# A last expert stage whose stored sums, bias, norms and buffers are arranged anew

## The chip, the cores and the metric

The program runs on one core of a Trainium2 chip. The core has TensorE (PE, matrix products into PSUM), VectorE (DVE), ScalarE (ACT), GpSimd (POOL) and SyncE (SP), each with an instruction queue of its own that it works through in order; they meet at semaphores, and data come and go by DMA, which here SP and POOL issue. The metric is the time of one execution on the device in microseconds (us), as the median of several runs. Before the change it is 5069.14 us, the median of 3 runs from 5067.45 to 5076.32.

## The reference

The input x is (2, 256, 64, 64), in two layers: a state-space scan block over 4096 tokens; then a forward and a backward scan block on normalised tokens, and a mixture of eight experts with a router. Only the end of it is touched:

```python
t = t + ffn(layer_norm(t))            # t: (2 batches, 4096 tokens, 256 channels)
# ffn(x):
feat = mean(x, axis=0)                # over the two batches
w = softmax(feat @ Wr + br)           # (tokens, 8), shared by the batches
h = relu(bn1(x @ W1[e] + b1[e]))      # for each of the 8 experts e
h = relu(bn2(h @ W2[e] + b2[e]))
y = h @ Wo[e] + bo[e]
ffn = sum over e of w[:, e] * y[e]
```

## The kernel before

**Tiling.** Tokens go in 8 chunks of T = 512 for each of 2 batches; channels lie in KC = 2 halves of 128 partitions. One [128, 2, 512] float32 tile (512 KB) is a chunk of one batch. A *pair* is (batch b, chunk i, expert e): three layers, each of 4 products of a 128x128 weight with 512 columns (8 matmul instructions in the profile).

**The scans (up to L1137).** A slot plan, written out by hand in `Slots`, gives every piece of work a slot and a queue; `in_order` ties each engine to the traced order. In the slots where PE and ACT have room, `experts` and `emit_experts` compute pairs ahead of time: the three layers of L989, evictions by ACT at L1000 and, for the last layer, the copy of L998 into a tile `eu`, which SP or, at the end, POOL stores to DRAM as `u` (L1019). `features` stores the normalised chunk as `nf_dram` (L891). Of the 128 pairs 86 are stored this way: all of batch 0, and in batch 1 chunks 7 and 6 whole and experts 0 to 5 of chunk 5 (`first[b, i]` is the number of stored experts). Only (batch 1, chunk 0) has no stored norm. The tiles of this work have the tags `ew0` to `ew2` (weights), `en`, `eh1`, `eh2` and `eu` in the pool `wk` of the scans.

**The last stage (from L1140)** opens new pools when those of the scans are closed: `mw` for the weights of all experts, `mk` for the rest, `ps_o` for the sums in PSUM, and four PSUM banks (`psm`) for all other products. It computes the 42 pairs that are left:

- `rest` lists the chunks that have pairs left, in order 4, 3, 2, 1, 0, 5 (8 pairs each, 2 in chunk 5); `whole` is 7, 6.
- The main loop (L1347) does a pair's first two layers (`layer`, L1283, evicted by ACT at L1287), multiplies the hidden tile of the pair before by the router's weights (`weigh`, DVE, L1294), and adds the last layer of the pair three before into PSUM (`last_layer`, L1302). After a chunk's last pair DVE adds PSUM to x (L1307) and SP stores it (L1257).
- `routes(i)` is the router of a chunk: `load_n` (POOL's DMA, L1168), `layer_norm` where no norm is stored, `both` (POOL adds the norms of both batches, L1190), `logits` (PE, L1197, then a softmax on DVE and ACT), `spread` (PE transposes, ACT copies, POOL stores the weights and loads them back over all partitions as `wb`, L1226 and L1228).
- `sums(i)`: load x (L1238); `bias`, a product of the router's weights with `bo` (L1245), copied by ACT (L1246) and added to x of both batches by POOL (L1248); then for each stored result a load (L1252), a product with `wb` (L1253) and an add to x (L1254), both on DVE.
- `side[i]` holds a chunk's stored sums and the routers of the chunks to come, dealt out evenly over that chunk's own pairs:

```python
upto = -(-len(work) // (count[i] - done[i] + 1))
for fn in work[:upto]:
    fn()
```

So chunk 5's 14 stored sums come with its two pairs, at the very end.

Of the kernel before, what the change touches and what calls it, by code (L numbers as in the profile page):

```python
# [134 lines left out]
def hybrid_kernel(ctx: ExitStack, tc: tile.TileContext, a: dict, out: bass.AP):  # L135
# [41 lines left out]
    wr = const.tile([P, KC, E], F32, name="wr")  # L177
    br = const.tile([P, E], F32, name="br")
# [10 lines left out]

    with ExitStack() as st:  # L190
# [7 lines left out]
        psp = st.enter_context(tc.tile_pool(name="psp", bufs=3, space=PSUM))  # L198
# [16 lines left out]
        def load_weights(job, tag, s0):  # L215
# [4 lines left out]
            def weight(key, home, shape, name):  # L220
# [4 lines left out]
                elif key == "x":  # L225
                    w["x_dt"] = wk.tile([P, KC * C], F32, tag="ew2", name=f"{name}_{tag}")
                    w[key] = w["x_dt"][:, : nj * XC].rearrange("p (j n) -> p j n", j=nj)
                else:
                    w[key] = wk.tile(shape, F32, tag=NARROW_W[home], name=f"{name}_{tag}")
# [226 lines left out]
        def prepare(i):  # L456
# [8 lines left out]
            def of_chunk(key, j, bufs, home):  # L465
                if not ahead:
                    ck[key, j] = wk.tile([P, T], F32, tag=key, name=f"{key}_{tag}_{j}", bufs=bufs)
                else:
                    if j == 0:
                        ck[key] = wk.tile([P, KC, T], F32, tag=home, name=f"{key}_{tag}")  # L470
# [11 lines left out]
            def scaled():  # L482
                ck["nx"] = wk.tile([P, KC, T], F32, tag="en", name=f"nx_{tag}")
# [6 lines left out]
            def load_x():  # L490
                ck["x"] = wk.tile([P, KC, T], F32, tag="eh1", name=f"x_{tag}")
# [407 lines left out]
        def scales():  # L899
# [3 lines left out]
            def load():  # L903
# [5 lines left out]
                nc.sync.dma_start(wr, a["Wr"].rearrange("(k p) e -> p k e", p=P))  # L909
                nc.sync.dma_start(br, a["br"].to_broadcast([P, E]))  # L910

            def shift():
# [5 lines left out]
                nc.vector.tensor_scalar(wr, wr, 1.0 / NB, None, ALU.mult)  # L918
# [63 lines left out]
        def emit_experts(put):  # L982
            ew, before = {}, {}

            def layer(x, dst, l, m, e, key):
# [8 lines left out]
                def act():  # L994
                    if dst not in key:
                        key[dst] = wk.tile([P, KC, T], F32, tag=f"e{dst}", name=f"e{dst}_{key['tag']}")
                    if l == 2:
                        nc.scalar.copy(key[dst][:, m, :], key["ps", l, m])  # L998
# [8 lines left out]
            def load_w(l, e, tag):  # L1007
                ew[l] = wk.tile([P, KC, C], F32, tag=f"ew{l}", name=f"ew{l}_{tag}")
# [4 lines left out]
            def load_n(b, c):  # L1013
                n[b, c] = wk.tile([P, KC, T], F32, tag="en", name=f"en_{b}{c}")
# [49 lines left out]
        def chunk_stats(n, s0):  # L1064
            v = {}

            def load():
                v["x"] = wk.tile([P, KC, T], F32, tag="eu", name=f"xst_{n}")
# [71 lines left out]
    with ExitStack() as st:  # L1140
# [3 lines left out]
        psp = st.enter_context(tc.tile_pool(name="psm", bufs=4, space=PSUM))  # L1144
# [11 lines left out]
        rest.sort(key=lambda i: sum(first[b, i] for b in range(NB)))  # L1156

        def load_n(i):

            if (0, i) in n:  # L1160
                return
            for b in range(NB):
                n[b, i] = mk.tile([P, KC, T], F32, tag="n", name=f"n_{i}{b}", bufs=6)
# [5 lines left out]

        def layer_norm(i):  # L1170
# [305 lines left out]
```

## Time and profile before

One execution was profiled. It lasted 5072.22 us, of which the span of the instructions is 5070.5 us.

| | us |
|---|---|
| median of the runs | 5069.14 |
| profiled execution / its span | 5072.22 / 5070.5 |
| busy in the span: PE, DVE, ACT, POOL | 4247.6, 4581.4, 3609.1, 4409.8 |
| last matmul of the scans' experts ends | 4504.4 |
| first matmul of the last stage | 4517.58 |
| busy 4518 to 4985 (467 us): PE, DVE, ACT, POOL | 442.84, 241.86, 138.72, 69.31 |
| busy 4985 to 5071 (86 us): PE, DVE, ACT, POOL | 54.75, 44.79, 12.12, 5.75 |
| stored sums, DVE: 86 products, 86 adds | 1.22 each, median |
| hidden tile times weights, DVE: 42 | 1.22 each, median |

The profile names an instruction by its line in the kernel, the engine, what it writes and reads (`out<-in`), and gives the idle time of its engine before it and who ended that. The page cuts the span into 40 slices of 127 us; each digit is the busy share of a slice in tenths. The last stage is the last four and a half of them.

### The profile page before, as it was taken

To read this page: it belongs to the slowest core of one execution; us is meant where nothing else is said; L and a number is where in the kernel's file an instruction comes from. 1 tells how busy PE (TensorE), PEld (TensorE's weight loads), DVE (VectorE), ACT (ScalarE), POOL (GpSimd) and SP (SyncE) were. 2 spreads that over 40 slices of the span, in tenths; PEclk is the share of its full clock that TensorE was granted. 3 is DMA by queue.
4 is the path that set the end of the run, shared out by engine and by line. 5 is a ranking of instruction groups with operands and counts; after the bars stand their busy time and mean duration, and the time that the engine had idled before them with its cause. 6 is when DMAs were issued, how large, how long until landed. Compare 5 with 4: busy or idle time off the path is not lost. (4 is left out here: it accounts for less than half of the span.)

```text
span 5070.5 us, 47370 instructions
## 1 busy us (share of the span) xinstructions
PE 4247.6 (84%) x14920; PEld 1478.8 (29%) x14920; DVE 4581.4 (90%) x3096; ACT 3609.1 (71%) x7319; POOL 4409.8 (87%) x1442
## 2 busy tenths in 40 slices
PE   5667787787777899989999888898868999888997
PEld 1222222222222333333333333333222333334443
DVE  6998999999999999999999999999999999946635
ACT  5677777777776877877787888878777788742231
POOL 5998999999999999999999999999999999931110
PEclk8788889899888999999999999999889999999998
DMA  5455444444444444457675555544444554544533
GB/s 189 155 172 180 160 159 160 146 155 155 170 167 155 162 171 165 160 198 246 233 243 185 175 184 178 188 161 172 140 160 167 175 177 158 175 168 175 199 112 137
DMA packets 333947, 873.15 MB, mean 172 GB/s; under 512 B 36408, under 2 KB 111936, under 8 KB 291712
## 3 DMA queue, kind: packets, MB, share of 16 engines
q1 hardware_dynamic: 329408, 842.73, 48.4%
q0 software_dynamic: 4288, 27.40, 1.4%
q8 instruction: 118, 1.93, 0.2%
q14 instruction: 133, 1.09, 0.1%
HBM read 671.17 MB, written 198.84 MB: 172 GB/s over the span
## 5 line engine op out<-in xcount | busy, mean ns | idle before, releaser
L737 POOL TENSOR_TENSOR bq<-rxdt,bc 128x2048 f32<-128x2048 f32 x640 | 2892.7, 4541 | 17.3 <-DMA rxdt<-xdtd 8.3
L747 ACT ACTIVATE da<-rdt,w_a 128x512 f32<-128x512 f32 x2560 | 1757.3, 686 | 110.3 <-DVE bq L773 63.9
L773 DVE TENSOR_TENSOR_SCAN da<-da,h_state,bq 128x1024 f32<-128x1024 f32 x664 | 1558.0, 2346 | 55.3 <-ACT da L747 44.7
L798 POOL TENSOR_TENSOR bq<-bq,bc 128x2048 f32<-128x2048 f32 (+1 forms) x280 | 1180.0, 4214 | 22.5
L773 DVE TENSOR_TENSOR_SCAN bq<-da,h_state,bq 128x1024 f32<-128x1024 f32 x456 | 1059.5, 2339 | 23.7 <-ACT da L747 23.7
L806 PE MATMUL y<-bq,stack 128*32 128x512 f32 x5120 | 741.9, 665 | 275.3 <-POOL bq L798 251.5
L782 DVE TENSOR_TENSOR bq<-da,bc 128x1024 f32<-128x1024 f32 x760 | 926.3, 1219 | 15.7
L989 PE MATMUL e<-eh,ew 128*128 128x512 f32 x1376 | 671.6, 622 | 63.9 <-DMA ew<-in_Wo 17.0
L792 ACT COPY h_state<-da 128x2 f32<-128x2 f32 x759 | 119.3, 157 | 634.1 <-DVE bq L782 632.3
L758 ACT ACTIVATE bq<-h_state,bq,a 128x1 f32<-128x1 f32 x1120 | 430.2, 384 | 2.7 <-POOL bq L737 2.0
L989 PEld LDWEIGHTS e<-eh,ew 128*128 128x128 f32 x1376 | 250.7, 194 | 475.9 <-issue 239.9
L806 PEld LDWEIGHTS y<-bq,stack 128*32 128x32 f32 x5120 | 140.1, 116 | 820.2 <-POOL bq L798 359.7
L450 PE MATMUL z<-nx,w_in 128*128 128x512 f32 x640 | 329.1, 643 | 58.1 <-DVE nx L414 21.2
L523 PE MATMUL conv<-xs,w_conv 64*64 64x512 f32 x2560 | 330.1, 602 | 23.5 <-ACT xs L507 21.3
L989 PE MATMUL e<-en,ew 128*128 128x512 f32 x688 | 323.8, 604 | 22.9 <-DVE fcen L886 15.8
L450 PE MATMUL xs<-nx,w_in 128*128 128x512 f32 x640 | 317.3, 625 | 21.1 <-DVE xc L536 7.9
L1287 ACT ACTIVATE h<-hp,of,sc 128x512 f32<-128x512 f32 x168 | 130.4, 777 | 252.2 <-PE hp L1283 235.6
L838 PE MATMUL o<-sz,w_out 128*128 128x512 f32 x640 | 298.3, 605 | 0.0
L1000 ACT ACTIVATE eh<-e,of,sc 128x512 f32<-128x512 f32 x344 | 259.3, 767 | 44.1 <-PE e L989 43.9
L590 POOL TENSOR_TENSOR xdt<-sp,xc 128x512 f32<-128x512 f32 x160 | 203.3, 1275 | 46.0 <-DVE sp L586 45.8
L773 DVE TENSOR_TENSOR_SCAN da<-da,bq 128x1024 f32<-128x1024 f32 x96 | 219.4, 2285 | 3.8 <-ACT da L747 2.2
L1248 POOL TENSOR_TENSOR x<-x,bi 128x1024 f32<-128x1024 f32 x16 | 37.2, 2338 | 188.8 <-DMA x<-t_dram 108.0
(141 smaller groups left out, 4924.1 us busy)
## 6 DMA issues: line engine op xcount, KB each, us to landing
rxdt<-xdtd SPq DMA_DIRECT2D x160, 1024.0 KB, 6.6
rdt<-dtd SPq DMA_DIRECT2D x160, 1024.0 KB, 6.5
bc<-bcd SPq DMA_DIRECT2D x384, 256.0 KB, 3.2
ew<-in_W SPq DMA_DIRECT2D x172, 256.0 KB, 5.0
u<-u SPq DMA_DIRECT2D x86, 512.0 KB, 4.3
u<-eu SPq DMA_DIRECT2D x82, 512.0 KB, 4.3
dtd<-sp SPq DMA_DIRECT2D x160, 256.0 KB, 3.5
xdtd<-xdt SPq DMA_DIRECT2D x160, 256.0 KB, 3.4
```

Source lines behind the costliest of these rows:

```text
L450: nc.tensor.matmul(ps, job.matrices["in", half][:, k, j * P : (j + 1) * P], rhs, start=(k == 0), stop=(k == KC - 1),)
L523: nc.tensor.matmul(v[r][64 * col : 64 * col + 64, :], job.matrices["conv"][rows, 2 * jp + j, k, :], ck["xs", jp][rows, j, k : k + T] if k ...
L737: nc.gpsimd.tensor_tensor(bq[g], ck["rxdt", j], over_groups(ck["bc", 0, sg]), ALU.mult)
L747: nc.scalar.activation(da[g, h][:, k, :], cks[i]["rdt", j][:, q, :], AF.Exp, scale=steps[i][0].w["a"][:, j, q * SG + sg : q * SG + sg + 1],)
L758: nc.scalar.activation(bq[g][:, q, 0:1], job.h[:, j, sg, q : q + 1], AF.Identity, scale=cks[i]["a0", j][:, h, sg : sg + 1], bias=bq[g][:, ...
L773: nc.vector.tensor_tensor_scan(b if on_pool(g, h) else d, d, b, job.h[:, j, sg, 2 * h : 2 * h + 1] if c else 0.0, ALU.mult, ALU.add,)
L782: nc.vector.tensor_tensor(bq[g][:, two, :], d, cks[i]["bc", 1, sg].rearrange("p (o t) -> p o t", o=1).to_broadcast([P, 2, T]), ALU.mult,)
L798: nc.gpsimd.tensor_tensor(b, b, cks[i]["bc", 1, sg].rearrange("p (o t) -> p o t", o=1).to_broadcast([P, groups, T]), ALU.mult,)
L806: nc.tensor.matmul(y[i, j][q * CG : (q + 1) * CG, :], stack, bq[g][:, q, :], start=False, stop=(sg == SG - 1),)
L838: nc.tensor.matmul(v[m], job.w["out"][:, j, m * P : (m + 1) * P], ck["sz", j], start=False, stop=(j == job.nj - 1),)
L989: nc.tensor.matmul(ps, ew[l][:, k, m * P : (m + 1) * P], key[x][:, k, :], start=(k == 0), stop=(k == KC - 1),)
L1000: nc.scalar.activation(key[dst][:, m, :], key["ps", l, m], AF.Relu, bias=of[:, l, e, m : m + 1], scale=sc[:, l, e, m : m + 1],)
```

## The change

Buffers: a pool `ep` and the PSUM pool `psp` (3 banks) are opened outside the scans and serve both parts. The tiles with the tags `ew*`, `en`, `eh*` and `eu` move into `ep` everywhere (one such line is shown). The last stage takes its stored results (`summand`), the sum of norms (tag `en`) and the last expert's weights (tags `ew*`) from these tiles; `layer` takes its three banks from `psp`, and the router's products share one bank (`psm`).

Output bias: at the eviction of a stored result, `bo` is added by ACT (`bo_col`). For pairs of the last stage, a product of the router's weights with `bo`, zero where an expert is stored, opens the sum in PSUM (`late_bias`). The step `bias` goes.

Sum of norms: except for the first chunk, it is loaded by POOL's DMA from `nf_dram` of one batch, and the other batch's is added by an accumulating DMA. Batch 0's norms are no longer loaded by themselves. `wr` and `br` are loaded in the last stage, on POOL's queue, not in the scans.

Order: `rest` becomes 4, 3, 2, 1, 5, 0. All stored sums stand in one list with costs (2.5 for a sum, 0.3 for a load of x) that is dealt out over all 42 pairs; routers stand in a second list, a step or two to a pair. x is loaded for one batch at a time, at its first sum, or before the add of PSUM. A chunk is stored once its last part is added. Weights are loaded three tiles to a pair, not six. `wb` has three buffers, not two.

```diff
+
+    ep = ctx.enter_context(tc.tile_pool(name="ep", bufs=1))
+    psp = ctx.enter_context(tc.tile_pool(name="psp", bufs=3, space=PSUM))
+    bo_col = const.tile([P, E, KC], F32, name="bo_col")
...
-                    w["x_dt"] = wk.tile([P, KC * C], F32, tag="ew2", name=f"{name}_{tag}")
+                    w["x_dt"] = ep.tile([P, KC * C], F32, tag="ew2", name=f"{name}_{tag}")
...
-                nc.sync.dma_start(wr, a["Wr"].rearrange("(k p) e -> p k e", p=P))
-                nc.sync.dma_start(br, a["br"].to_broadcast([P, E]))
+                nc.sync.dma_start(bo_col, a["bo_col"])
...
-                        key[dst] = wk.tile([P, KC, T], F32, tag=f"e{dst}", name=f"e{dst}_{key['tag']}")
+                        key[dst] = ep.tile([P, KC, T], F32, tag=f"e{dst}", name=f"e{dst}_{key['tag']}")
                     if l == 2:
-                        nc.scalar.copy(key[dst][:, m, :], key["ps", l, m])
+                        nc.scalar.activation(
+                            key[dst][:, m, :], key["ps", l, m], AF.Identity, bias=bo_col[:, e, m : m + 1]
+                        )
...
-        psp = st.enter_context(tc.tile_pool(name="psm", bufs=4, space=PSUM))
+        psm = st.enter_context(tc.tile_pool(name="psm", bufs=1, space=PSUM))
...
-        rest.sort(key=lambda i: sum(first[b, i] for b in range(NB)))
+        rest.sort(key=lambda i: (len([b for b in range(NB) if (b, i) not in featured]), sum(first[b, i] for b in range(NB))))
...
         def load_n(i):
 
-            if (0, i) in n:
-                return
             for b in range(NB):
-                n[b, i] = mk.tile([P, KC, T], F32, tag="n", name=f"n_{i}{b}", bufs=6)
+                if first[b, i] == E and i != rest[0]:
+                    continue
+                n[b, i] = mk.tile([P, KC, T], F32, tag="n", name=f"n_{i}{b}", bufs=4)
                 if (b, i) in featured:
                     src = nf_dram[b][:, i, :, :]
                 else:
                     src = t_dram[b][:, :, i * T : (i + 1) * T]
                 nc.gpsimd.dma_start(n[b, i], src)
 
+        def summand(name):
+            homes.append(homes.pop(0))
+            return ep.tile([P, KC, T], F32, tag=homes[-1], name=name)
+
+        homes = ["eh1", "eh2", "eu"]
...
             for b in range(NB):
-                if (b, i) in featured:
+                if (b, i) in featured or (b, i) not in n:
...
         def both(i):
-            n["sum", i] = mk.tile([P, KC, T], F32, tag="nm", name=f"nm_{i}", bufs=1)
-            nc.gpsimd.tensor_tensor(n["sum", i], n[0, i], n[1, i], ALU.add)
+            n["sum", i] = ep.tile([P, KC, T], F32, tag="en", name=f"nm_{i}")
+            if i == rest[0]:
+                nc.gpsimd.tensor_tensor(n["sum", i], n[0, i], n[1, i], ALU.add)
+                return
+            alone = [b for b in range(NB) if (b, i) in featured]
+            for b in alone:
+                nc.gpsimd.dma_start(
+                    n["sum", i], nf_dram[b][:, i, :, :],
+                    accum_op=ALU.bypass if b == alone[0] else ALU.add,
+                )
+            for b in range(NB):
+                if b not in alone:
+                    nc.gpsimd.tensor_tensor(n["sum", i], n["sum", i], n[b, i], ALU.add)
...
-            wb[i] = mk.tile([P, E, T], F32, tag="wb", name=f"wb_{i}")
+            wb[i] = mk.tile([P, E, T], F32, tag="wb", name=f"wb_{i}", bufs=3)
...
         def routes(i):
-            return [lambda: load_n(i), lambda: layer_norm(i), lambda: both(i), lambda: logits(i), lambda: spread(i)]
-
+        def load_x(b, i):
+            if (b, i) in x:
+                return
+            x[b, i] = mk.tile([P, KC, T], F32, tag="x", name=f"x_{i}{b}", bufs=6)
+            nc.sync.dma_start(x[b, i], t_dram[b][:, :, i * T : (i + 1) * T])
 
         def add_early(b, i, e):
-            u = mk.tile([P, KC, T], F32, tag="u", name=f"u_{b}{i}_{e}", bufs=3)
+            u = summand(f"u_{b}{i}_{e}")
...
+        left = {}
+
+        def added(b, i):
+            left[b, i] -= 1
+            if not left[b, i]:
+                store(b, i)
+
         def sums(i):
 
-            work = [lambda: load_x(i), lambda: bias(i)]
+            work = []
             for b in range(NB):
-                work += [lambda b=b, e=e: add_early(b, i, e) for e in range(first[b, i])]
-                if first[b, i] == E:
-                    work.append(lambda b=b: store(b, i))
+                left[b, i] = first[b, i] + (first[b, i] < E)
+                for e in range(first[b, i]):
+                    if not e:
+                        work.append((0.3, lambda b=b: load_x(b, i)))
+                    work.append((2.5, lambda b=b, e=e: (add_early(b, i, e), added(b, i))))
             return work
 
-        bo = mw.tile([E, C], F32, name="bo")
-        we = {}
-        order = sorted(range(E), key=lambda e: e < first[NB - 1, rest[0]])
+        def late_bias(k):
+            if k not in bo:
+                bo[k] = mw.tile([E, C], F32, name=f"bo_{k}")
+                if k:
+                    nc.vector.memset(bo[k], 0.0)
+                nc.sync.dma_start(bo[k][k:, :], a["bo"][k:, :])
+            return bo[k]
+
+        bo, we = {}, {}
+        order = list(range(E))
+        order = order[first[NB - 1, rest[0]] :] + order[: first[NB - 1, rest[0]]]
+        kept = [(name, e) for e in order[-1:] for name in ("W1", "W2", "Wo")]
...
@@ -1297,15 +1327,21 @@
             begins, ends = (e == [p[2] for p in pairs if p[:2] == (b, i)][k] for k in (0, -1))
             if begins:
                 y[b, i] = ps_o.tile([P, KC, T], F32, tag="y", name=f"y_{i}{b}")
+                for m in range(KC):
+                    nc.tensor.matmul(
+                        y[b, i][:, m, :], late_bias(first[b, i])[:, m * P : (m + 1) * P], wts[i],
+                        start=True, stop=False,
+                    )
             for m in range(KC):
                 for k in range(KC):
                     nc.tensor.matmul(
                         y[b, i][:, m, :], we["Wo", e][:, k, m * P : (m + 1) * P], h[:, k, :],
-                        start=(begins and k == 0), stop=(ends and k == KC - 1),
+                        start=False, stop=(ends and k == KC - 1),
                     )
             if ends:
+                load_x(b, i)
                 nc.vector.tensor_tensor(x[b, i], y[b, i], x[b, i], ALU.add)
-                store(b, i)
+                added(b, i)
...
+        chunks = rest[:1]
+        for k in range(max(len(rest), len(whole))):
+            chunks += rest[k + 1 : k + 2] + whole[k : k + 1]
+        starts_at = {i: min(k for k, p in enumerate(pairs) if p[1] == i) for i in rest}
+        ends_at = {i: max(k for k, p in enumerate(pairs) if p[1] == i) for i in rest}
+        ahead = [(cost, fn, i) for i in chunks for cost, fn in sums(i)]
+        total = sum(item[0] for item in ahead)
+        todo = [(i, fn) for i in chunks[1:] for fn in routes(i)]
+
+        load_n(chunks[0])
+        wr = mw.tile([P, KC, E], F32, name="wr")
+        br = mw.tile([P, E], F32, name="br")
+        nc.gpsimd.dma_start(wr, a["Wr"].rearrange("(k p) e -> p k e", p=P))
+        nc.gpsimd.dma_start(br, a["br"].to_broadcast([P, E]))
+        nc.vector.tensor_scalar(wr, wr, 1.0 / NB, None, ALU.mult)
...
-        nc.sync.dma_start(bo, a["bo"])
+        late_bias(first[NB - 1, rest[0]])
         layer_norm(rest[0])
         both(rest[0])
-        for i in whole[:1] + rest[1:2]:
+        for i in rest[1:2]:
...
+        weighed, loaded = -1, [2]
+
+        def free(i):
+
+            k = chunks.index(i) - 3
+            if k < 0:
+                return True
+            old = chunks[k]
+            return all(item[2] != old for item in ahead) and ends_at.get(old, -1) <= weighed
+
+        def load_ahead(at):
+            while loaded[0] < len(rest):
+                old = rest[loaded[0] - 2]
+                if ends_at[old] >= at or ("sum", old) not in n:
+                    break
+                load_n(rest[loaded[0]])
+                loaded[0] += 1
+
+        def route_on():
+            i, fn = todo[0]
+            if i in rest and not any((b, i) in n for b in range(NB)):
+                return False
+            if len(todo) > 1 and todo[1][0] == i or free(i):
+                fn()
+                todo.pop(0)
+                return True
+            return False
+
+        def finish_route(i):
+            while i not in wb:
+                if not route_on():
+                    if ahead[0][2] in wb:
+                        ahead.pop(0)[1]()
+                    else:
+                        weigh_next()
+
+        def weigh_next():
+            nonlocal weighed
+            weighed += 1
+            b, i, e = pairs[weighed]
+            finish_route(i)
+            weigh(b, i, e, hs[weighed])
+
+        hs, spent = {}, 0.0
         for at, (b, i, e) in enumerate(pairs):
-            for name, k in weights[: 6 if at else 4]:
+            for name, k in weights[: 3 if at else 4]:
                 load_w(name, k)
-            weights = weights[6 if at else 4 :]
+            weights = weights[3 if at else 4 :]
+            if at and i != rest[0]:
+                finish_route(i)
             h = layer(n[b, i], 0, e, f"{i}_{e}_{b}")
-            h = layer(h, 1, e, f"{i}_{e}_{b}")
+            hs[at] = layer(h, 1, e, f"{i}_{e}_{b}")
             if at == 0:
                 logits(i)
             elif at == 1:
                 spread(i)
-
-            for p in {0: [], 1: [], 2: waiting[:1], 3: waiting[1:]}.get(at, waiting[-1:]):
-                weigh(*p)
-            waiting.append((b, i, e, h))
-            if len(waiting) > 3:
-                last_layer(*waiting.pop(0))
-            done[i] += 1
-            work = side[i] if at > 1 else []
-            upto = -(-len(work) // (count[i] - done[i] + 1))
-            for fn in work[:upto]:
+            while weighed < at - 1 and at > 1:
+                weigh_next()
+            if at > 2:
+                last_layer(*pairs[at - 3], hs[at - 3])
+            load_ahead(at + 1)
+            if at < 2:
+                continue
+            if todo:
+                route_on()
+            target = total * (at - 1) / (len(pairs) - 4)
+            while ahead and spent < target and ahead[0][2] in wb:
+                cost, fn, _ = ahead.pop(0)
                 fn()
-            side[i] = side[i][upto:]
-        weigh(*waiting[-1])
-        for p in waiting:
-            last_layer(*p)
+                spent += cost
+            if todo and (todo[0][0] in rest and starts_at[todo[0][0]] < at + 6 or len([c for c in chunks if c in wb]) < 3):
+                route_on()
+        while weighed < len(pairs) - 1:
+            weigh_next()
+        for at in range(max(0, len(pairs) - 3), len(pairs)):
+            last_layer(*pairs[at], hs[at])
+        while ahead or todo:
+            load_ahead(len(pairs))
+            if todo:
+                route_on()
+            while ahead and ahead[0][2] in wb:
+                ahead.pop(0)[1]()
         in_order()
 
```

## The prediction

> **What bounds the kernel now.** I read the 40 slices of the page first, then the last stage by stretches, then TensorE's instructions in order of time, then who waited for whom. Up to the last three slices DVE and POOL stand at 9 and over (the scans); then PE alone does.
>
> ```profile
> PE   5667787787777899989999888898868999888997
> DVE  6998999999999999999999999999999999946635
> POOL 5998999999999999999999999999999999931110
> ```
>
> The change rewrites the last stage, so I need that stage's own sum. The stretches (us, then busy time and instructions of each engine, granted clock, DMA share, GB/s):
>
> ```profile
> 4505.00:4518.00 13.00, 0.42 (x1) 0.45 (x2) 0.00 (x0) 0.00 (x1) 2.22 (x4) 0.61 0.74 250
> 4518.00:4985.00 467.00, 442.84 (x1094) 195.14 (x1094) 241.86 (x234) 138.72 (x189) 69.31 (x50) 0.97 0.47 168
> 4985.00:5071.00 86.00, 54.75 (x115) 22.27 (x113) 44.79 (x36) 12.12 (x17) 5.75 (x4) 0.80 0.41 147
> ```
>
> In the middle PE is busy 442.8 of 467 us; around it lie a hole of 13 us and an end where PE has 31 us free. The timeline (start, length, instruction, idle time before it and who ended it) shows the hole, one full pair, and the end:
>
> ```profile
> 4493.64 10.74 PE L989 MATMUL e<-eh,ew 128*128 128x512 f32 x24
> 4517.58 5.57 PE L1283 MATMUL hp<-n,W 128*128 128x512 f32 x8 [13.20 <-DMA n<-nf_dram]
> ...
> 5000.46 3.60 PE L1283 MATMUL hp<-n,W 128*128 128x512 f32 x8
> 5003.90 3.87 PE L1283 MATMUL hp<-h,W 128*128 128x512 f32 x8
> 5007.61 3.60 PE L1302 MATMUL y<-h,Wo 128*128 128x512 f32 x8
> ...
> 5035.11 6.23 PE L1302 MATMUL y<-h,Wo 128*128 128x512 f32 x8 [7.79 <-DVE h L1294]
> 5059.01 6.23 PE L1302 MATMUL y<-h,Wo 128*128 128x512 f32 x8 [17.67 <-DVE h L1294]
> ```
>
> A pair (batch, chunk, expert) costs PE 10.58 us from its first matmul to the next pair's. The last chunk has two pairs and 14 stored results to add, so PE waits 7.79 and 17.67 us for DVE. After a hole the same eight matmuls take 5.6 to 6.2 us instead of 3.6.
>
> PE from 4504.4 (end of the scans' last expert) to 5065.2: 42 pairs x 10.58 = 444.4; router logits 8 x 1.70 = 13.6; transposes 8 x 0.44 = 3.5; bias matmuls 8 x 1.92 = 15.4; one layer norm 3.9. Work 480.8. Nine holes: 13.20 + 10.99 + 1.65 + 1.65 + 4.84 + 2.22 + 2.40 + 7.79 + 17.67 = 62.4. Slow matmuls after the five holes over 4 us: 2.1 + 4.5 + 3.3 + 2.6 + 2.6 = 15.1. Together 558.3 of 560.9; the rest of 2.6 I keep. From PE's end the last add and store take 5.2, to 5070.5.
>
> **Part 1, output bias at eviction, in the scans.** A copy of ACT gets a bias operand.
>
> ```profile
> L998 ACT COPY eu<-e x172: 559/578/587, 1662.8 to 4504.4; 128x512 f32<-128x512 f32 x172
> L558 ACT ACTIVATE dbc_rows<-dbc,one_row x48: 663/667/682, 39.5 to 4316.4; 64x512 f32<-64x512 f32 x48
> ```
>
> L558 is the same instruction (Identity, bias column, out of PSUM): +89 ns x 172 = 15.3 us of ACT, queued ahead of the next `da`. ACT is busy 2277 of 2880 us there, and DVE is the engine that waits for it: of DVE's idle time in the scans 73.7 us end at ACT, but only 17 of those waits (19.6 us) have an L998 in the 5 us before. 17 x 0.09 = **+1.5**; bounds 0 and +15.3 (cover gone everywhere). Loading `bo_col` in place of `wr` and `br` is one issue for two: 0.
>
> **Part 2, pools shared with the scans: the hole at 4504.** Before, even the first weight load (SP at 4508.58) and the first `n` load (POOL at 4509.15) waited until the last `eu` store had landed at 4508.2, because the stage's pool lies over the scans' pool as a whole. After, `eu` lives in the outer pool; what is left there ends with the `xr` store, issued 4494.45, about 3.1 to landing: weights can start at 4498. The `n` loads still stand behind the last `eu` store on POOL's queue (issued 4505.29, 0.53 long): first issue 4505.9, second 4506.4. An `n` load lands in 3.8/8.5/13.4 us; it shares the DMA with weights and `u` loads, as before, but most weights have gone, so I take 6.6: PE starts at 4513. Hole 8.6 instead of 13.2; bounds 5.8 and 15.4. `wr` and `br` come behind the `n` loads on POOL and have PE's first pair (9 us) to land.
>
> **Part 3, fewer PE steps.** Bias goes into PSUM for 6 (batch, chunk) sums instead of 8 chunks: 6 x 1.92 = 11.5, **-3.8**. POOL loses 16 adds of 2.34 and six of some 2.7; they were off PE's path except where they made PE wait (the 10.99 and 4.84 holes, both at `nm`). Work now 476.9.
>
> **Part 4, stored sums spread.** Following the new loop by hand, the chunk order is 4, 3, 2, 1, 5, 0: the last chunk now has eight pairs, and the 86 sums come 2 or 3 to a pair, done at pair 39 of 41. DVE per pair: 2.3 x 2.44 + 1.22 = 6.8 of 10.6 us; `weigh` of a pair is used two pairs later, which covers 20 us of lateness. So the two end holes (25.5) and their slow matmuls (5.2) go, and so do 10.99 + 4.84 with 7.8 of slow matmuls.
>
> **Part 5, what is late next.** Walking each queue pair by pair I find these waits of PE:
> - *Sum of norms by DMA, chunks 3 and 7.* POOL can issue it only behind the `wb` load of the chunk before (4542.6 before, now 4.5 earlier: 4538.1), and PE asks for it in pair 3, at 4551.4. No accumulating DMA is in the trace; the nearest row is `n<-nf_dram`, 8.5 median for the same 512 KB. By the row alone, both at once, it is there by 4548 and costs nothing. [...] two in series, 17.5 us, there at 4556.2, PE stalls 4.8. No run here shows it. [...] 4.8 in pair 3, 3.3 in pair 5 (the second queues behind the first chunk's `wb`), as against 0 by the row. A sum of 29 us or more would stall four chunks; the others have over 20 us to spare.
> - *Logits and transposes in one pair* (3, 5, 19, 32). The loop now emits both behind each other, so PE idles for the softmax, 1.65 in the two such holes of the trace: 4 x 1.65, plus 2 in pairs 3 and 32 for DVE's queue and 1.5 slow clock: about 10.
> - *Layer norm of chunk 0:* 2.40 as before, and 1.3 because the matmul outputs now have three banks, which fill while ACT takes the root.
> - *The zero-filled bias of chunk 5, pair 35.* `late_bias(6)` is first called there: a memset on DVE, then a load on SP, then PE's matmul. On DVE the memset stands behind: the add of `y` of chunk 1, which ends where PE ends pair 34 (call it 0); two stored sums whose loads stand on SP behind the store of that add (issue 1.8, land 6.1 at 4.3 median, done 11.0); `weigh` 12.2. Memset 12.4, load (2.8, as the 16 KB row `w_dram`) 15.2. PE is there at 7.15: hole **8.0** and 2.6 slow. Bounds 0 (if the loads were ahead) and 14.
>
> Stalls: 4.8 + 3.3 + 10 + 3.7 + 10.6 = 32.4.
>
> **Sum.** 4504.4 + 8.6 + 2.1 (slow start) + 476.9 + 2.6 + 32.4 = 5027.0; end 5.2 and scans 1.5: **5033.7** against a span of 5070.5, so -36.8. The profiled execution lasted 5072.2, 3.1 above the median of the runs, with 1.7 outside the span; nothing outside changes. I take the difference off the median: 5069.1 - 36.8 = **5032**.
>
> **Rivals.**
> - *The new waits are hidden.* Accumulation no slower than the row, bias in time: 32.4 - 8.1 - 10.6 leaves 13.7; 5032 - 19 = 5013. For it: SP runs ahead wherever buffers are free. Against: the store ahead of those loads waits for PE itself.
> - *The scans pay.* All 15.3 us of ACT arrive on DVE's path: 5032 + 14 = 5046. For it: `DVE da` waits for `ACT da`, 30 us in 42 waits of the later scans. Against: only 17 waits follow an eviction.
> - *Slower: accumulating DMAs.* Place: the logits of chunks 3, 7, 6 and 1 on PE. Slack from POOL's issue to PE's need: 13, 15, 21 and 23 us. At 40 us a sum: 27 + 25 + 19 + 17 = 88, less the 8.1 counted: +43 over before. It decides from about 30 us a sum, 15 a DMA against 8.5 for a plain one.
> - *The pools don't free earlier* (a leftover of the scans holds the memory): the hole stays 13.2, 5036; inside the range.
>
> **Chances.** Forecast with its parts within their bounds 0.58 (5021 to 5042 on its own), hidden waits 0.23, scans pay 0.12, accumulating DMAs 0.04, something unseen 0.03. Range 5006 to 5050: from below the hidden case with an early start, to the scans' case. A difference under 0.2% (10 us) can't be told from no change; faster 0.93, same 0.03, slower 0.04.
>
> **What would show it.** Start of the first `hp` matmul near 4513; the end without holes over 3 us and PE at 9 in the last slice; PE idle before the bias matmul of pair 35, ended by the load of `bo_6`; PE idle before the logits of chunks 3 and 7; L998 near 667 ns with the scans' end within 2 us of 4504. Wrong if the scans end later by 10 us or more, or if DVE, not PE, fills the stage.

## The result and the profile after

The median goes from 5071.64 us (four runs, 5067.45 to 5076.32) to **5034.49** (four runs, 5033.81 to 5034.88): ratio 0.9923, 95% interval 0.9908 to 0.9939, so 37 us. The profiled execution lasted 5034.19, its span 5032.4. The forecast was 5032, and 5033.7 for the span.

First the slices of after: the share of busy time of TensorE (PE), DVE and POOL in 40 equal parts, in tenths.

```profile
PE   5777778788777899989999998989868899889998
DVE  6998999999999999999989999999999999955654
POOL 5998999999999999999999999999999999950000
```

PE now carries the last slices as it did the ones before them (9 and 8, where the last two had 9 and 7); in the one 8 at the very end lie the hole of pair 35, below, and the 5.2 us after PE's last product. DVE's last five are 5, 5, 6, 5, 4 where they were 4, 6, 6, 3, 5: the same sums, more evenly dealt. POOL has 0 in its last four, where it had 1, 1, 1, 0. The same stage by stretches (us, busy time and instructions of PE, weight loads, DVE, ACT, POOL, then granted clock, DMA share, GB/s):

```profile
4505.00:4518.00 13.00, 3.13 (x4) 1.51 (x5) 1.90 (x1) 0.00 (x0) 5.71 (x7) 0.57 1.03 357
4518.00:4950.00 432.00, 414.81 (x1023) 182.00 (x1022) 242.96 (x245) 123.05 (x165) 23.16 (x34) 0.96 0.56 193
4950.00:5033.00 83.00, 77.14 (x175) 32.35 (x173) 30.78 (x26) 18.65 (x24) 0.00 (x0) 0.99 0.24 82
```

The end is full (77.1 of 83 us), at a granted clock of 0.99 where it was 0.80. The start is nearly as empty as before (3.1 of 13 us), but its DMA share has gone from 0.74 to 1.03: the memory is free earlier, and the bytes that now come earlier come together. The middle is busy for 415 of 432 us; its gaps stand in TensorE's timeline (start, length, instruction, then the idle time before it and who ended it):

```profile
4492.58 10.74 PE L988 MATMUL e<-eh,ew 128*128 128x512 f32 x24
4514.87 6.47 PE L1313 MATMUL hp<-n,W 128*128 128x512 f32 x8 [11.55 <-issue]
...
4554.08 1.85 PE L1215 MATMUL lt<-wr,nm 128*128 128x8 f32 x16
4557.67 0.69 PE L1240 MATMUL wt<-ident,w 128*8 128x128 f32 x4 [1.74 <-DVE w L1234]
4558.15 5.25 PE L1313 MATMUL hp<-n,W 128*128 128x512 f32 x8
...
4941.09 3.75 PE L1331 MATMUL y<-wts,bo 8*128 8x512 f32 x4 [7.41 <-DMA bo<-in_bo]
4944.76 6.57 PE L1337 MATMUL y<-h,Wo 128*128 128x512 f32 x8
...
5013.31 13.90 PE L1337 MATMUL y<-h,Wo 128*128 128x512 f32 x32
```

Four things are to be seen. The hole at the stage's start is 11.55 us, 1.65 less than before; the profile names no releaser for it (`issue`), but the second norm landed at 4514.78, 0.09 us before it ends. The logits of chunk 3 (4554.08) start without a wait, then 1.74 us pass for the softmax, and the eight matmuls behind take 5.25 instead of 3.60. The zero-filled bias of pair 35 lets PE wait 7.41, and it and the matmuls behind it run slowly (3.75 for 1.98, 6.57 for 3.60). The last products are 32 matmuls on end, with no hole in them.

Because the end of the scans alone moves between 4501 and 4512 us from one profile to the next, though their program hardly differs, I compare below the **stage's length**, from the end of the scans' last expert product to the end of the span: 566.1 before, 529.1 after (525.4 in a second profile of after, `e10_after_again`). This 3.7 lies in slow matmuls: the second profile has none behind the softmax hole of pair 19 and behind the layer norm, 2.8 and 1.7 us in the first. The last section shows such matmuls behind one hole and not behind its like; a difference of a few us between two stages can be that alone.

### The profile page after: what moved, and what is told of

It reads as the page before. It is cut to its first block, busy times and chain, and to the rows that moved or that the text cites. A ratio compares the mean times of both kernels' runs of the same rounds, so it can differ in the third digit from the quotient of the medians.

```text
span 5032.4 us, 47312 instructions
## 1 busy us (share of the span) xinstructions
PE 4249.7 (84%) x14912; PEld 1477.5 (29%) x14912; DVE 4569.8 (91%) x3097; ACT 3614.0 (72%) x7303; POOL 4361.3 (87%) x1426
## 5 line engine op out<-in xcount | busy, mean ns | idle before, releaser
L783 DVE TENSOR_TENSOR bq<-da,bc 128x1024 f32<-128x1024 f32 x760 | 927.1, 1220 | 15.7
L814 PE MATMUL y<-xc,w_d 128*128 128x512 f32 x320 | 186.6, 667 | 20.0 <-DVE sz L820 19.8
```

The lines of the kernel that those rows point to most:

```text
L783: nc.vector.tensor_tensor(bq[g][:, two, :], d, cks[i]["bc", 1, sg].rearrange("p (o t) -> p o t", o=1).to_broadcast([P, 2, T]), ALU.mult,)
```

## The experiments

Each is after with one edit, unless said. Medians are of four runs unless said; ratios are to runs of before on the same chip. After itself came to 0.9923 on one chip and 0.9908 on another, so ratios from different chips that differ by this little say nothing. Stages are compared with the 529.1.

### Was the work evenly dealt?

`e4_old_deal` takes the old chunk order and gives each chunk's sums to its own pairs again:

```diff
-rest.sort(key=lambda i: (len([b for b in range(NB) if (b, i) not in featured]), sum(first[b, i] for b in range(NB))))
+rest.sort(key=lambda i: sum(first[b, i] for b in range(NB)))
...
+        group = {i: sum(c for c, _, j in ahead if j == i or j in whole[k - 1 : k] * (k > 0)) for k, i in enumerate(rest)}
+        earlier = {i: sum(group[j] for j in rest[:k]) for k, i in enumerate(rest)}
...
-            target = total * (at - 1) / (len(pairs) - 4)
+            target = earlier[i] + group[i] * (at - starts_at[i] + 1) / (ends_at[i] - starts_at[i] + 1)
```

> The chunks go in the old order and each chunk's stored sums are dealt to its own pairs, as before; all else as in the changed kernel. Theory (spreading the sums is the main gain): chunk 5's 14 sums again meet two pairs, PE waits 7.8 and 17.7 us for DVE at the end and runs slowly after each, about 30 us, less some 12 for the bias tile of chunk 5 whose wait lies in the same stretch: 5052 to 5065. Rival (the gain came from the bias step leaving POOL, so that the sums begin earlier): under 5042.

Measured: 5060.6 us (nine runs, 5057.54 to 5068.01), ratio 0.9977 [0.9967, 0.9987]; the stage is 23.5 longer. TensorE's timeline of this run:

```profile
4764.03 1.01 PE L1240 MATMUL wt<-ident,w 128*8 128x128 f32 x4 [14.04 <-DVE w L1234]
...
5038.28 3.75 PE L1331 MATMUL y<-wts,bo 8*128 8x512 f32 x4 [21.19 <-DMA bo<-in_bo]
```

The stored sums stand on DVE in bulk again: at the end the memset of the zero-filled bias is behind them, and PE waits 21.19 us; in the middle the softmax is, and PE waits 14.04. The bias is only the last in that queue: the last pair's `weigh` ends on DVE at 5034.21, behind the same sums. So dealing the sums out in order is what took the end holes away. It is not what took the `nm` holes of before (10.99 and 4.84) away: with the old deal no wait for a norm sum comes back.

`e5_old_order` takes back the chunk order alone (the first of the two edits):

> Only the order of the chunks is the old one (chunk 5 last); the sums are dealt over all pairs. Theory (the dealing matters, the order little): 5025 to 5037; the bias tile of chunk 5 is then loaded at the very end behind little on DVE, so some of its 12 us may go. Rival (chunk 5 must not be last): the last two pairs are starved as before, 5050 or more.

Measured: 5026.01 (5024.77 to 5030.18), 0.9907 [0.9892, 0.9922], stage 518.6. This run and `e4_old_deal`, on one chip, differ in the dealing alone: 34.6 us. The new order isn't needed, and may cost something (8 us between the medians, with intervals that overlap, and 0.9908 for the second group of runs of after): with the old one the bias hole is 4.21 instead of 7.41, and one softmax hole is missing, since the last chunk's logits and transposes fall into different pairs. Of the 10.5 us of stage, 4.5 are the slow matmuls of pair 19 and of the layer norm, missing here as in the second profile of after.

### Do the earlier loads come from the shared pools?

`e2_pools_apart` opens the expert tiles' pool and the PSUM pool inside the scans' stack and opens new ones in the last stage, so that nothing is shared:

```diff
-    ep = ctx.enter_context(tc.tile_pool(name="ep", bufs=1))
-    psp = ctx.enter_context(tc.tile_pool(name="psp", bufs=3, space=PSUM))
     with ExitStack() as st:
+        ep = st.enter_context(tc.tile_pool(name="ep", bufs=1))
+        psp = st.enter_context(tc.tile_pool(name="psp", bufs=3, space=PSUM))
...
     with ExitStack() as st:
+        ep = st.enter_context(tc.tile_pool(name="ep2", bufs=1))
+        psp = st.enter_context(tc.tile_pool(name="psp2", bufs=3, space=PSUM))
```

> The shared pools are closed with the scans and opened again for the last stage, so its memory lies over the scans' as before. Theory (POOL's queue and the landing of the norms set the start; sharing brings only the wait for the last store of eu): weights start near 4508, the first product of the stage moves from 11.5 to about 13.2 us after the scans' last one, 5036 to 5037. Rival (the early weights are what the stage lives on): the hole grows to 17 us or more and the first pairs wait for weights too, 5040 and over.

Measured: 5033.67, 0.9924 [0.9909, 0.9939]; hole 11.69, first weight load at 4497.69. The theory falls: the weights start as early as in after without any sharing. `e11_one_pool` then puts the expert tiles back into the scans' own pool `wk`:

```diff
-    ep = ctx.enter_context(tc.tile_pool(name="ep", bufs=1))
...
-        wk = st.enter_context(tc.tile_pool(name="wk", bufs=1))
+        wk = ep = st.enter_context(tc.tile_pool(name="wk", bufs=1))
...
         mk = st.enter_context(tc.tile_pool(name="mk", bufs=2))
+        ep = st.enter_context(tc.tile_pool(name="ep", bufs=1))
```

> In the scans the experts' tiles lie among the other tiles of the scans' pool, as before the change; the last stage opens a pool of its own for the tiles it took from them, behind its others. With the pools merely closed and opened again (the second run) the weights still started at 4497.7, so sharing itself brought nothing there. Theory (what counts is that the weights' memory does not lie over the pool that holds eu): the weights and norms wait for the last store of eu again, first weight 3 us after that store is issued, hole 13 us instead of 11.5, total within 5 us of the changed kernel's 5032 to 5034. Rival (the weights' early start comes from something else in the change): weights again start some 7 us before the last store of eu is issued, hole 11 to 12 us.

Measured: 5033.84 (5028.51 to 5035.93), 0.9925 [0.9907, 0.9942]. POOL's timeline of this run shows the last `eu` store and the loads of the first norms:

```profile
4502.27 0.53 POOL L1019 DMA_DIRECT2D u<-eu  x1 [6.61 <-ACT eu L996]
4506.11 1.06 POOL L1169 DMA_DIRECT2D n<-nf_dram  x2 [3.31 <-DMA u<-eu]
```

The wait for the store's landing is back (3.31), and the first weights went out at 4505.55, 4.3 us behind the scans' last expert product; in after, at 4496.75, 6.6 ahead of it. So the separate pool did free the memory, as I had read it. But the hole is 11.89, against 11.55 and 11.63 in the two profiles of after: **the freed 11 us are worth next to nothing to PE** (the expectation had 13 us for this hole). They are given back on the way: the two norms land 4.47 and 6.16 us after their issue here, 7.30 and 8.36 in after. The stretches in which they travel, of after, then of `e1_bias_first`, where SP happens to stand still and sends nothing beside them (columns as above):

```profile
4506.00:4515.00 9.00, 0.13 (x1) 0.16 (x1) 0.00 (x0) 0.00 (x0) 2.30 (x5) 0.55 1.05 355
```

```profile
4503.50:4510.00 6.50, 0.04 (x1) 0.07 (x1) 0.00 (x0) 0.00 (x0) 2.54 (x5) 0.74 0.72 244
```

In after all 16 engines are full (1.05, 355 GB/s) with weights, `x` and `u` that nobody waits for yet, and the norms are among them; with 244 GB/s they land in 4.63 and 5.38. That the other loads slow the norms is what this pair says; how much of it is theirs stays open, since before, with weights and norms issued as closely as in `e11_one_pool`, took 6.30 and 7.56.

`e8_sp_norms` has SP load the first norms, ahead of the weights and past POOL's queue with its `eu` store:

```diff
-                nc.gpsimd.dma_start(n[b, i], src)
+                (nc.sync if i == rest[0] else nc.gpsimd).dma_start(n[b, i], src)
```

> The first chunk's norms are loaded from SP's queue, ahead of the weights, not from POOL's behind the last store of the scans. Theory (their landing alone sets the start): they land by about 4502, PE goes from the scans' last product at 4503 straight on, the hole of 11.55 us and 2.9 us of slow matmuls go, about 5020. Rival (weights or memory hold the start as well, or the router's weight, still on POOL, holds the first logits): at most half of it, 5027 or more.

Measured: 5024.9 (5018.22 to 5028.53), 0.9902 [0.9887, 0.9917]; the stage is 12.3 shorter, some 2.8 of it slow matmuls that are missing behind softmax holes. TensorE's timeline:

```profile
4508.94 3.67 PE L1313 MATMUL hp<-n,W 128*128 128x512 f32 x8 [2.19 <-DMA W<-in_W]
```

The norms go out at 4500.19, 6.6 us ahead of the scans' last product, where in after they went out 2.6 behind it. The hole falls to 2.19, and the eight matmuls take 3.67. What the rival named is there, but small: the 2.19 end at a weight, and the first logits wait 0.70 for `wr`. So the start was a matter of when the norms are issued; the edit changes their queue and their place ahead of the weights at once, and what each of the two is worth wasn't tried.

### What does the bias at eviction cost?

`e3_copy` takes the plain copy again (it leaves out the output bias of the stored results):

```diff
-                        nc.scalar.activation(
-                            key[dst][:, m, :], key["ps", l, m], AF.Identity, bias=bo_col[:, e, m : m + 1]
-                        )
+                        nc.scalar.copy(key[dst][:, m, :], key["ps", l, m])
```

> The stored results are evicted by a plain copy, without their output bias. Theory (the 90 ns that each of 172 evictions takes longer lie in ACT's idle time): 5033 to 5035, no difference. Rival (they delay the decays that DVE waits for): all of 15 us comes back, 5020.

Measured: 5035.17 (5023.03 to 5042.4), 0.9922 [0.9904, 0.9940], stage 529.1. No difference. In after the row of this line (count, then ns at least, median and at most, first and last start) is

```profile
L997 ACT ACTIVATE eu<-e,bo_col x172: 665/669/690, 1662.6 to 4504.1; 128x512 f32<-128x512 f32 x172
```

so 91 ns more in each of 172, 15.7 us of ACT that lie beside DVE's work. The scans' expert products end at 4503.31, a microsecond before the old end; within the spread of that end, 1.5 us can't be told from nothing.

### The zero-filled bias

`e1_bias_first` builds both biases at the stage's start:

```diff
-        late_bias(first[NB - 1, rest[0]])
+        for i in rest:
+            late_bias(first[NB - 1, i])
```

> Both bias tiles are filled at the start of the last stage; nothing else differs from the changed kernel (5034.5 us). Theory (PE waits in pair 35 for nothing but the memset and the load of the second bias tile): the hole of 7.41 us and some 4.8 us of slow matmuls after it go, about 5022. Rival (the weighed tile or the stored sums on DVE are as late as the bias): PE stops there all the same, 5030 to 5034.

Measured: 5018.17, ratio 0.9896 [0.9878, 0.9914]; the four runs lie in two groups, 5011.6 twice and 5025 twice, and what divides them is left open. The profile is of the faster group. TensorE's timeline of the profiled execution (5011.56):

```profile
4509.97 5.40 PE L1313 MATMUL hp<-n,W 128*128 128x512 f32 x8 [8.15 <-issue]
...
4923.07 1.98 PE L1331 MATMUL y<-wts,bo 8*128 8x512 f32 x4
```

The bias product has no idle time before it and takes 1.98: the hole and the slow matmuls after it, 12.1 us, are gone (the granted clock of after was 0.62 from 4936 to 4954). The stage is 21.1 shorter, more than that, because a side effect came with it: the second bias is memset by DVE behind the scaling of `wr`, and SP waits for that memset 15.69 us with the remaining weights behind it. That is the empty stretch shown above; the hole at the start is 3.4 shorter. The rest is slow matmuls, 3.0 less behind the softmax holes and 1.7 less behind the layer norm. Nothing in the edit asks for that; it is of the size by which the two profiles of after differ.

In after, DVE's timeline shows why the hole is there:

```profile
4926.57 1.23 DVE L1343 TENSOR_TENSOR x<-y,x 128x1024 f32<-128x1024 f32 x1 [2.08 <-PE y L1337]
4933.38 1.23 DVE L1262 TENSOR_TENSOR u<-u,wb 128x1024 f32<-128x1024 f32 x1 [5.58 <-DMA u<-u]
...
4938.17 1.22 DVE L1324 TENSOR_TENSOR h<-h,wb 128x1024 f32<-128x1024 f32 x1
4939.38 0.27 DVE L1292 MEMSET bo<- 8x256 f32 x1
```

The add of `y` waits for PE; its result's store holds SP, and the load of `u` behind it, so DVE idles 5.58; two sums and a weighing later comes a memset of 0.27 us, and then its load.

### Logits and transposes in one pair

`e7_logits_apart` does not take the second routing step of a pair where the first or second was the logits, so that the transposes come a pair later:

```diff
+            step = len(todo) % 4
             if todo:
                 route_on()
...
-            if todo and (todo[0][0] in rest and starts_at[todo[0][0]] < at + 6 or len([c for c in chunks if c in wb]) < 3):
+            if todo and (step, len(todo) % 4) not in ((3, 2), (2, 1)) and (todo[0][0] in rest and starts_at[todo[0][0]] < at + 6 or len([c for c in chunks if c in wb]) < 3):
```

> A chunk's norm sum, logits and transposes are never dealt to the same pair as one another. Theory (PE waits 1.74 us for the softmax in four pairs and runs slowly after it): four holes and their slow matmuls go, 4 x (1.74 + 1.7) = 14 us, about 5021. Rival (the slow matmuls come from the narrow logits products, not from the hole behind them): only the holes go, 7 us, about 5027.

Measured: 5026.23 (5024.88 to 5031.55), 0.9909 [0.9894, 0.9923], stage 9.7 shorter: between the two. TensorE's timeline:

```profile
4560.99 1.85 PE L1215 MATMUL lt<-wr,nm 128*128 128x8 f32 x16
4562.69 3.68 PE L1313 MATMUL hp<-n,W 128*128 128x512 f32 x8
...
4596.31 1.92 PE L1215 MATMUL lt<-wr,nm 128*128 128x8 f32 x16 [1.20 <-DMA nm<-nf_dram]
```

All four holes are gone, and behind the logits the matmuls take 3.68, so the narrow products alone slowed nothing here: the rival's reason falls. The 14.4 us of after (holes 7.0, slow matmuls 7.4) went, but 7.1 came back: PE now reaches pair 35 earlier while DVE doesn't (the hole there is 11.54, +4.1), and it waits 1.20 for a sum of norms, with 1.8 of slow matmuls behind. That leaves 7.3 of the 9.7; most of the rest is the slow stretch behind the layer norm (1.6), which is missing here. The ratio alone, that of the second group of runs of after, would not show the gain; on this run's chip `e2_pools_apart` and `e3_copy`, which gain nothing, took 5033.67 and 5035.17. The rival's time was near for another reason.

### Do the accumulating DMAs cost anything?

POOL's timeline of after, for chunk 3:

```profile
4538.14 0.53 POOL L1202 DMA_DIRECT2D nm<-nf_dram  x1
4546.38 0.90 POOL L1202 DMA_DIRECT2D nm<-nf_dram  x1 [7.71 <-DMA nm<-nf_dram]
```

The second, accumulating DMA waits 7.71 us for the first one's landing: two in series, as the prediction took them. But it lands 5.30 us after its issue (5.3 to 7.6 in all six), faster than the plain ones ahead of them (7.9 to 15.7), which travel beside the 2 MB load of `wb`. The sum is there at 4551.68, and PE asks at 4554.08: no stall.

`e6_pool_sum` loads both norms plainly and lets POOL add them:

```diff
-            for b in alone:
-                nc.gpsimd.dma_start(
-                    n["sum", i], nf_dram[b][:, i, :, :],
-                    accum_op=ALU.bypass if b == alone[0] else ALU.add,
-                )
-            for b in range(NB):
-                if b not in alone:
-                    nc.gpsimd.tensor_tensor(n["sum", i], n["sum", i], n[b, i], ALU.add)
+            nc.gpsimd.dma_start(n["sum", i], nf_dram[0][:, i, :, :])
+            if (1, i) not in n:
+                n[1, i] = mk.tile([P, KC, T], F32, tag="n1w", name=f"n1w_{i}", bufs=1)
+                nc.gpsimd.dma_start(n[1, i], nf_dram[1][:, i, :, :])
+            nc.gpsimd.tensor_tensor(n["sum", i], n["sum", i], n[1, i], ALU.add)
```

> The norms are summed by POOL's adds of two plain loads, not by an accumulating DMA; the bias step stays away. Theory (the holes of 10.99 and 4.84 us at the norm sum came from POOL standing in the bias step for loads of x, not from the add): no hole comes back, 5032 to 5037. Rival (the DMA sum is what removed them): some 16 us of holes and 8 of slow matmuls return, about 5058.

Measured: 5036.29, 0.9924 [0.9907, 0.9940], stage 530.6. The `nm` holes of before (10.99 and 4.84) don't come back with POOL's add, so the DMA sum didn't remove them, and by `e4_old_deal` the dealing didn't either (the softmax hole of pair 3 grows from 1.74 to 3.68). POOL's timeline of before, ahead of the 10.99 us hole that ends at 4681.49:

```profile
4673.53 4.63 POOL L1248 TENSOR_TENSOR x<-x,bi 128x1024 f32<-128x1024 f32 x2 [51.82 <-DMA x<-t_dram]
4678.12 3.32 POOL L1190 TENSOR_TENSOR nm<-n,n 128x1024 f32<-128x1024 f32 x1
```

The norm sum stands behind the bias step, and that behind a load of `x`. This step is gone in after, `e4_old_deal` and `e6_pool_sum` alike, and is the cause that remains; it wasn't tried alone.

### All that helped, together

`e9_all` joins `e1_bias_first`, `e7_logits_apart` and `e8_sp_norms`; `e10_after_again` is after itself, beside it.

> Bias tiles at the stage's start, router steps in pairs of their own and the first norms on SP's queue, all three together. Theory (the three waits are separate pieces of PE's path and add up): from the changed kernel's 5034.5 us go 12.2 for the bias tile, 13.6 for the softmax holes and 12.2 at the start, 4997 us; the stage is then PE's own work with the layer norm's hole. Rival (a removed hole is refilled by DVE being as late as PE): 5005 or more.

> The changed kernel once more, beside the one with all three edits, on the same chip: 5034.5 us as before if the chip plays no part; another value tells how far single medians of the other runs can be trusted (they spread by 4 to 19 us).

Measured: **5004.02** (5001.51 to 5006.71), 0.9857 [0.9842, 0.9871], beside 5031.78 for after (0.9908 [0.9891, 0.9924]): 27.8 less than after, the fastest kernel of this study, and 7 above the 4997 of the expectation. The middle is PE's nearly alone, 427.02 of 432 us, as the stretch of this run (columns as above) says:

```profile
4518.00:4950.00 432.00, 427.02 (x1060) 186.10 (x1060) 252.31 (x251) 127.73 (x171) 23.17 (x34) 0.99 0.60 207
```

The three edits alone shortened the stage by 21.1, 9.7 and 12.3, 43.1 together, and joined by 33.3. TensorE's timeline shows part of the difference:

```profile
4546.22 2.30 PE L1215 MATMUL lt<-wr,nm 128*128 128x8 f32 x16 [1.25 <-DMA nm<-nf_dram]
4548.37 6.68 PE L1313 MATMUL hp<-n,W 128*128 128x512 f32 x8
```

With PE earlier everywhere the norm sums, free in after, are late twice (1.25 and 0.84), and 3.5 us of slow matmuls follow; `e1_bias_first` and `e8_sp_norms` had also taken the same hole at the start, and all three had been credited with missing slow matmuls that nothing in the edits asks for.

## Why the prediction was right

The total is right to 1.3 us of span, but **not because each term was**, and the scans' end alone moves by 10 us between profiles: that closeness is luck. As span, term by term (forecast, then after's profile):

| term | forecast | measured | difference |
|---|---|---|---|
| scans' last expert product ends | 4505.9 | 4503.3 | -2.6 |
| hole at the start, slow matmuls after it | 8.6 + 2.1 | 11.55 + 2.9 | +3.7 |
| waits for the norm sums, pairs 3 and 5 | 8.1 | 0 | -8.1 |
| softmax holes, slow matmuls after them | 10 | 7.0 + 7.4 | +4.4 |
| layer norm of chunk 0 | 2.4 + 1.3 | 2.5 + 1.6 | +0.4 |
| zero-filled bias, slow matmuls after it | 8.0 + 2.6 | 7.4 + 4.7 | +1.5 |
| work 476.9, tail 5.2, what was kept (2.6); measured: the remainder | 484.7 | 484.1 | -0.6 |

- **Sums spread (part 4): right for the end holes, and shown** by undoing it (`e4_old_deal`). Both `nm` holes went as forecast, but not by the spreading, to which part 4 gave them: they stay away without it. I had said PE would stand at 9 in the last slice; it is 8, since the hole of pair 35 and the tail fall into it, 13.2 of 126 us by my own figures.
- **Shared pools (part 2): the reading of the waits was right, the price wrong.** Weights at 4498 and norms at 4505.9 were forecast, 4496.75 and 4505.89 came. The step that failed is "most weights have gone, so I take 6.6": SP, free earlier, ran on into later weights, `x` and `u`, and the norms landed after 8.4. The step's effect on PE is nil, as `e11_one_pool` shows; the 1.65 us less of hole can't be credited to it.
- **Norm sums (part 5): the order was right, the size wrong.** Two in series was an assumption of mine that no run before the change had shown; POOL shows it in after (7.71 us of wait for the first's landing). The term mis-sized is the landing of the accumulating DMA, 8.5 in my sum, 5.3 measured in pair 3. PE also asks later than I had it, at 4554.08 and not 4551.4, for the later start (4514.87, not 4513) and the slow matmuls behind it; the forecast stall of 4.8 became 2.4 us to spare, and in `e9_all`, where PE is earlier, the waits are there (1.25 and 0.84). This makes the "new waits are hidden" rival true for one of its two halves: the norm sums are hidden, the bias is not. The rival that they are dear (40 us a sum) is far off.
- **Softmax holes: right in their four places,** 1.74 each; what I under-counted is the slow matmuls after them, taken as 1.5 in all and 7.4 measured (5.1 in the second profile of after). The 2 us for DVE's queue in pairs 3 and 32 didn't come.
- **Zero-filled bias: right in place, cause and size.** DVE's order was as worked out, add, two sums behind a store, weigh, memset. Only the slow matmuls after it cost more (4.7 for 2.6).
- **Bias at eviction: right,** 91 ns for the 89 of the row, and hidden (`e3_copy`). The rival that the scans pay falls.
- **Layer norm:** the 1.3 for three PSUM banks didn't show; 1.6 of slow matmuls stood in its place.
- **The slices:** the prediction lets DVE and POOL stand at 9 up to the last three of them; by its own rows they do so up to the last five. No sum rests on it.

So the forecast is right through the largest gain, named and shown, and through errors that cancel: -11.3 in three terms, of which -8.1 are the norm sums, and +10.0 in four. Had the accumulating DMA been taken by its row, the forecast would have been 5024, still in the range but 10 us out.

## What to carry to other kernels

When buffers come free earlier, ask which loads will now start and what they share the DMA with: here the urgent load gained next to nothing from free memory (hole 11.55 us, 11.89 without it), while being issued first, from another queue, took 9 us off the hole (2.19). A tiny instruction (a memset of 0.27 us) placed where it is first needed inherits the whole queue ahead of it, store and all; put it where no one waits. After one wait is taken away, walk the same queue again from PE's new, earlier times: the norm sums, free in after, were late again as soon as other holes closed (1.25 and 0.84 us in `e9_all`).

## What the runs showed of the hardware

**The granted clock after a short hole: lower in some cases, not in others.** Two stretches of after around the logits of chunk 3 (granted clock is the third number from the end):

```profile
4548.00:4556.00 8.00, 7.93 (x30) 4.04 (x28) 7.44 (x8) 0.78 (x1) 0.00 (x0) 1.00 0.92 248
4556.00:4566.00 10.00, 8.32 (x18) 3.61 (x19) 9.47 (x14) 2.93 (x5) 1.61 (x3) 0.83 0.80 278
```

The clock falls from 1.00 to 0.83, with a hole of 1.74 us in the second stretch. Slow matmuls came behind all four softmax holes of after, but behind two of four in `e1_bias_first` and three of four in the second profile of after, and not behind before's like hole of 1.65, after which eight matmuls took 3.60. Here is pair 19, first in after, where the granted clock was 0.57 from 4745 to 4753, then in `e1_bias_first`:

```profile
4743.42 1.85 PE L1215 MATMUL lt<-wr,nm 128*128 128x8 f32 x16
4747.01 1.01 PE L1240 MATMUL wt<-ident,w 128*8 128x128 f32 x4 [1.74 <-DVE w L1234]
4747.82 5.98 PE L1313 MATMUL hp<-n,W 128*128 128x512 f32 x8
```

```profile
4737.19 1.85 PE L1215 MATMUL lt<-wr,nm 128*128 128x8 f32 x16
4740.78 0.60 PE L1240 MATMUL wt<-ident,w 128*8 128x128 f32 x4 [1.74 <-DVE w L1234]
4741.21 3.60 PE L1313 MATMUL hp<-n,W 128*128 128x512 f32 x8
```

The logits (1.85) and the hole (1.74) are the same in both; behind them the four transposes take 1.01 in after and 0.60 in `e1_bias_first`, the eight matmuls 5.98 and 3.60. What divides the two isn't shown. A softmax hole cost 1.4 to 3.0 us of slow matmuls, or none; where no hole follows the logits (`e7_logits_apart`, chunk 3) the eight matmuls behind them take 3.68.

**An accumulating DMA into SBUF was no dearer than a plain load:** 512 KB landed 5.3 to 7.6 us after issue, the plain loads ahead of them, beside the 2 MB load of `wb`, in 7.9 to 15.7, and the plain loads of the first two norms in 4.5 to 9.2 (before, after, its second profile, `e1_bias_first`, `e2_pools_apart`, `e11_one_pool`).
